# Layer 1's expert results taken back batch by batch inside layer 2's causal attention, and the norms of five attentions computed with GpSimd's power

## The chip, the cores and the metric

The kernel runs on one core of one Trainium2 chip. The metric is the device time of one launch in microseconds, as the median of several runs, and less is better. Each engine of the core (TensorE or PE for matmuls, VectorE or DVE, ScalarE or ACT, GpSimd or POOL, SyncE or SP for DMAs) works off its own instruction queue in order; engines wait for each other through semaphores.

## What is computed

The reference is a post-norm decoder of four layers on `x` of 8 batches x 256 tokens x 256 features, with a context of 8 x 120 x 192. Each layer has a self attention, a cross attention and a feed-forward part, and after each of the twelve parts the residual is added and normalised:

```python
def _layernorm(x, axis=-1, eps=1e-05):
    m = jnp.mean(x, axis=axis, keepdims=True)
    v = jnp.var(x, axis=axis, keepdims=True)
    return (x - m) / jnp.sqrt(v + eps)
...
x = _layernorm(x + _L1_ffn_ref(x, ...), axis=-1)
x = _layernorm(x + _L2_attn_ref(x, ...), axis=-1)
```

Two parts matter here. `_L1_ffn_ref` is a mixture of 32 experts: every token goes to its 4 best experts (256 places each), and gets back the sum of their 4 results times the gate's weights, plus a shared expert's result. `_L2_attn_ref` is a causal attention with 16 heads of 16 features, whose keys and values come from a latent of 64 features behind an exact GELU. The other parts are an attention and cross attentions of other kinds, an expert layer with 8 experts, one with product keys and a table of 4096 experts, a gated convolution, and a feed-forward part on fixed-point numbers (`_L3_ffn_ref`).

## The kernel before

All of `x` stays on the chip as `X`, [128 partitions, 16 tiles, 256]: tile t holds tokens of batch t // 2, so a batch is two tiles. `xT` is its transpose, which the projections read. The twelve parts run one after the other as methods of `Net` (`l0_attn`, `l0_xattn`, `l0_ffn`, `l1_attn`, ... `l2_ffn`; layer 3's parts lie inside `l2_ffn`, the last of them being `fixed_point`, L1438). `build` calls each part's `load_...` one part ahead, so that its weights arrive during the part before, in one of two weight buffers that take turns.

The code states one order of the work. A scheduler in the build places each instruction into its engine's queue, by the program's order and its own estimate of when operands are ready; so the queue order on each engine is fixed before the launch, and where a few parts of the code are independent it can interleave them. Tiles come from pools with a set number of buffers, and a new use of a buffer waits for the readers of the old one.

**The norm.** `finish` (L159) calls `finish_x` (L165) for two tiles, and then `transpose_into_xT` (L150: four PE transposes and an ACT copy). `finish_x` takes mean and variance by `norm_stats` (L141; bn_stats L146 and bn_aggr L147 on DVE), then `rsqrt` (L126), then writes X as (z - mean) * r (L170, DVE). `rsqrt` is an approximation on DVE: add eps (L129), a first guess by integer arithmetic on the float's bits (L131), and three Newton steps of three instructions each (L134, L135, L137). That is eleven DVE instructions on 128x2 elements, each reading the one before. There are 104 norms of two tiles in the program.

**Layer 1's experts (`l1_ffn`, L971).** The gate's scores are ranked, and every token gets four places `slot` and weights `gw` (up to L1039). Each expert then gathers its 256 tokens from DRAM, computes and writes its result to the DRAM tensor `yd` by SP's DMA queue (L1054). In between, `prepare_l2_xattn` puts work of layer 2's cross attention here, including partition all-reduces on POOL. The take-back is the loop after it: for each of 16 tiles a matmul of the shared expert, `acc` = that + X (L1062, DVE), and four gathers of 128 rows of `yd` by `slot` (`gather_rows` L832, an indirect DMA whose descriptors POOL makes, L834) into `yg`, six buffers deep; after each gather DVE adds the row times its weight (L1067). After two tiles, `finish`.

**Layer 2's attention (`l2_attn`, L671, and the `attention16` family).** `attn16_pools` (L374) makes the value buffers `vp` and the row-maximum buffers `low` and fills them by POOL memsets (L384, L387). `attention16` (L571) projects batches in pairs (`pair`, L578: queries, the latent with GELU, keys and values by `project16` L610 and `values16` L405). For each batch, `largest16` (L434) computes scores on PE and reduces them to row maxima on DVE (short rows L445, long rows L461), `lower16` (L474) transposes the maxima and folds them into the queries (L482, DVE), `exps16` (L486) computes the transposed scores and their exponentials (ACT), `sums16` (L538) multiplies by the values and `divided16` (L518) divides; then `project_out` (L561) multiplies by `wo`, adds X plus bias (`biased`, L558, made by POOL, 128x512) into `z` (L566, DVE) and calls `finish_x`. The row maxima of batch b+1 are interleaved with the exponentials of batch b. `l1_xattn` and `l1_attn` use the same functions.

Of the kernel before, what the change touches and what calls it, by code (L numbers as in the profile page):

```python
# [11 lines left out]
F32 = mybir.dt.float32  # L12
BF16 = mybir.dt.bfloat16
I32 = mybir.dt.int32
U32 = mybir.dt.uint32
# [5 lines left out]
P = 128  # L21
# [21 lines left out]
class Net:  # L43
    def __init__(self, ctx: ExitStack, tc: tile.TileContext, ins, out):
# [40 lines left out]
        nc.scalar.dma_start(self.gate1, ins["l1f_gate"].rearrange("p (c n) -> p c n", c=2))  # L85
        self.avg = self.const.tile([P, 2, B], F32, name="avg")
        self.w_scale = self.const.tile([P, len(L2X)], F32, name="w_scale")
        self.wset = 0


# [6 lines left out]
        o, n = LAYOUT.consts[name]  # L97
        return self.consts[:, o : o + n]

    def load(self, *specs, rows=(), flat=None):  # L100
# [4 lines left out]
        total = sum(src.shape[1] for src in srcs) + sum(n for _, n in brow)  # L105
        whole = self.wpool.tile([P, total], F32, name=f"w{self.wset}")
        out, o = [], 0
        for (name, kc), src in zip(specs, srcs):
            part = whole[:, o : o + src.shape[1]]
            self.nc.sync.dma_start(part, src)  # L110
            out.append(part.rearrange("p (c n) -> p c n", c=kc))
            o += src.shape[1]
        for at, n in brow:
            self.nc.sync.dma_start(whole[0:1, o : o + n], self.ins["rows"][:, at : at + n])
            out.append(whole[0:1, o : o + n])
            o += n
        return (out, whole) if flat else out

    def mm(self, out, pairs, bias=None, m=P):
# [4 lines left out]
            self.nc.tensor.matmul(out, lhsT=self.ones[:, :m], rhs=bias, start=False, stop=True)  # L124

    def rsqrt(self, var, n):  # L126
        nc, tmp = self.nc, self.tmp
        v = tmp.tile([P, n], F32, name="rs_v")
        nc.vector.tensor_scalar(v, var, LN_EPS, None, ALU.add)  # L129
        y = tmp.tile([P, n], F32, name="rs_y")  # L130
        nc.vector.tensor_scalar(y.bitcast(I32), v.bitcast(I32), -0.5, 1597463007.0, ALU.mult, ALU.add)  # L131
        for _ in range(3):
            a = tmp.tile([P, n], F32, name="rs_a")
            nc.vector.scalar_tensor_tensor(a, y, -0.5, y, ALU.mult, ALU.mult)  # L134
            nc.vector.tensor_tensor(a, a, v, ALU.mult)  # L135
            y2 = tmp.tile([P, n], F32, name="rs_y")
            nc.vector.scalar_tensor_tensor(y2, a, 1.5, y, ALU.add, ALU.mult)  # L137
            y = y2
        return y
# [231 lines left out]

    def attn16_pools(self, ctx, name, size, nkb):  # L374
        tc, nc = self.tc, self.nc
        pool = ctx.enter_context(tc.tile_pool(name=name, bufs=1))
        work = ctx.enter_context(tc.tile_pool(name=name + "w", bufs=2))
        self.banks = [(ctx.enter_context(tc.tile_pool(name=name + "p", bufs=6, space=PSUM)), "sc")] * 6
        self.banks += [(self.ps_t, "pt")] * 2
        self.next_bank = 0  # L380
        low, vps = [], []
        for n in range(2):
            t = pool.tile([size, 2, nkb, 384], F32, name=f"vp{n}")
            nc.gpsimd.memset(t, 1.0)  # L384
            vps.append(t)
            t = pool.tile([P, 2, 2, P], F32, name=f"low{n}")
            nc.gpsimd.memset(t, 0.0)  # L387
            low.append(t)
        return work, low, vps

# [177 lines left out]

        return project_out, lambda: self.transpose_into_xT(2 * b, 1)

    def attention16(self, project, low, vps, sizes, causal, wo, bo, work):  # L571

# [5 lines left out]
        def pair(b):  # L578
            qv, kv = project(b, vps[b // 2 % 2])
            for n in range(2):  # L580
                q[b + n], k[b + n] = qv[:, :, :, n * S : (n + 1) * S], kv[:, :, :, n * width : (n + 1) * width]

        pair(0)
# [80 lines left out]


    def load_l2_attn(self):
        return self.load(
            ("l2a_wq", 2), ("l2a_wkd", 2), ("l2a_wku", 1), ("l2a_wo", 2), rows=("l2a_bku", "l2a_bo")
        )

    def l2_attn(self, w):  # L671
        nc = self.nc
        wq, wkd, wku, wo, bku, bo = w
        with ExitStack() as ctx:
            work, low, vps = self.attn16_pools(ctx, "a2", P, 2)
            bku, bo = self.everywhere(bku, work, "bku"), self.everywhere(bo, work, "bo")

            def project(b, vp):
# [12 lines left out]
                    self.values16(vp[:, n // 2, n % 2, :], pv, P, bku)  # L691
                return qv, kv

            self.attention16(project, low, vps, [P, P], True, wo, bo, work)

# [275 lines left out]
    def l1_ffn(self, w):  # L971
# [4 lines left out]
        with (  # L976
# [9 lines left out]
            gw = keep.tile([P, NT, K], F32, name="gw")  # L986
            slot = keep.tile([P, NT, K], U32, name="slot")
# [30 lines left out]
            yd = dram.tile([DROP + 1, D], F32, name="yd")  # L1018
# [132 lines left out]
    def l2_ffn(self, w):  # L1151
# [3 lines left out]
        with ExitStack() as ctx:  # L1155
# [760 lines left out]
```

## Time and profile before

| | |
|---|---|
| median of 3 runs | 2713.8 us (2710.76 to 2717.37) |
| the profiled execution | 2858.3 us, of which the profile's span is 2856.3 us |
| busy in the span | PE 2197.9 us (77%), DVE 1778.5 (62%), ACT 929.6 (33%), POOL 843.6 (30%) |
| mean granted TensorE clock | 0.867 of full speed |
| instructions | PE 14323, DVE 6270, ACT 2125, POOL 850 |
| POOL's gathers of `yg` (two expert layers) | 80, 78.4 us, 979 ns each |

The profile is one execution with the profiler on, so it is longer than the runs. A row of instructions gives the line, the engine, the operation, the tiles as out<-in with partitions x elements, the count, and then busy time and the mean of one; what stands after that is the idle time of the engine just before, and in "<-" what ended it. "issue" means that the engine waited for nothing that the profile shows. In a timeline each line is one instruction or several alike, with its start, its length, and in square brackets the idle time before it. The chain of waits is followed back from the last instruction: each line is the piece of work that the next one waited for.

In times of the profile, layer 0's attention runs to about 215 us, its cross attention to 315, its experts to 612, layer 1's attention to 815, its cross attention to 965, its experts to 1330 (routing to 1069, the experts themselves to 1229, then the take-back), layer 2's attention to 1540, its cross attention to 1706, the table experts with layer 3's first parts to 2650, and the fixed-point part to 2856.

### The profile page before, as it was taken

The page shows a single profiled execution, that of the slowest core. Times are in us where ns is not written, and L with a number is a line of the kernel's source. Part 1 is how long each engine was busy: PE and PEld are TensorE (multiplying, and loading weights), DVE is VectorE, ACT ScalarE, POOL GpSimd, SP SyncE. Part 2 cuts the span into 40 slices and gives each one's busy share as a digit, 9 for nine tenths or more (in the row PEclk, how much of TensorE's full clock was granted, in tenths as well). Part 3 has the DMA queues.
Part 4 walks back from the last instruction along what each step waited for, and adds up shares of the span by engine and source line. Part 5 has one row for each costly group of instructions (what it writes and reads, how often), then busy time and mean ns, then how long its engine had stood idle before and what let it go on. Part 6 is the DMA issues. An engine that isn't in the chain of part 4 may idle for free.

```text
span 2856.3 us, 41312 instructions
## 1 busy us (share of the span) xinstructions
PE 2197.9 (77%) x14323; PEld 1590.8 (56%) x14332; DVE 1778.5 (62%) x6270; ACT 929.6 (33%) x2125; POOL 843.6 (30%) x850
## 2 busy tenths in 40 slices
PE   8967587869988858835886667678787787777887
PEld 5544476735555547723554345456576675555665
DVE  4674400066667877445777887476586685755778
ACT  2321132323333302202442153235344344343442
POOL 1010021131111103454010015665656655663000
PEclk9988598989998959967998887789899898888899
DMA  2001266610001015731001011111111111120000
GB/s 79 2 1 37 100 244 238 249 36 1 1 15 53 16 45 153 214 102 45 1 1 56 1 45 34 47 43 40 48 38 45 47 39 38 50 74 19 1 12 19
DMA packets 84175, 166.31 MB, mean 58 GB/s; under 512 B 31654, under 2 KB 51254, under 8 KB 80256
## 3 DMA queue, kind: packets, MB, share of 16 engines
q0 software_dynamic: 52288, 110.52, 12.8%
q1 hardware_dynamic: 26746, 47.35, 5.0%
q10 hardware_dynamic: 4934, 5.82, 0.6%
q8 instruction: 114, 1.87, 0.3%
q14 instruction: 93, 0.76, 0.1%
HBM read 242.90 MB, written 17.70 MB: 91 GB/s over the span
## 4 chain that ended last, share of the span: by engine, by line
PE 24%; DVE 16%; issue 6%; another core or an unknown queue 3%; ACT 2%; POOL 1%; DMA 0%; POOLq 0%; DVEq 0%; ACTq 0%
PE po L1266 5%; PE pp L122 4%; PE s L122 4%; PE po L122 2%; DVE low L461 1%; PE s L1412 1%; PE po L1247 1%; PE s L1390 1%; PE sc L122 1%; DVE junk L1214 1%; POOL rows L834 1%; DVE low L445 1%; PE sc L428 1%; DVE X L170 1%
## 5 line engine op out<-in xcount | busy, mean ns | idle before, releaser
L834 POOL DMA_INDIRECT rows<-in_l2f_table_dram,index x512 | 530.0, 1035 | 364.2 <-issue 107.0
L1266 PE MATMUL po<-rows,diag 128*128 128x256 f32 x768 | 233.3, 441 | 95.4 <-ACT diag L1265 68.1
L1214 DVE SCALAR_TENSOR_TENSOR junk<-rows,X 128x256 f32<-128x256 f32 x512 | 214.9, 420 | 52.5 <-DMA rows<-in_l2f_table_dram,index 25.8
L1266 PEld LDWEIGHTS po<-rows,diag 128*128 128x128 f32 x768 | 156.9, 218 | 147.3 <-ACT diag L1265 80.5
L122 PE MATMUL pp<-xT,w 128*128 128x256 f32 (+1 forms) x672 | 195.6, 432 | 39.6 <-issue 25.3
L122 PE MATMUL ph<-xeT,we 128*128 128x128 f32 x1248 | 188.5, 296 | 41.1 <-DMA we<-in_l0f_experts_dram,wrow 35.9
L122 PEld LDWEIGHTS ph<-xeT,we 128*128 128x128 f32 x1248 | 175.0, 206 | 63.8 <-DMA we<-in_l0f_experts_dram,wrow 39.3
L536 POOL TENSOR_TENSOR aT<-sides,inv 128x256 f32<-128x256 f32 x64 | 46.8, 731 | 518.6 <-DVE sides L534 294.2
L122 PEld LDWEIGHTS pp<-xT,w 128*128 128x128 f32 x672 | 139.9, 215 | 74.4 <-issue 34.4
L156 PE MATMUL pt<-ident,X 128*128 128x128 f32 x352 | 78.1, 337 | 128.5 <-DVE X L170 86.8
L1265 ACT ACTIVATE diag<-ident,dots 128x128 f32<-128x128 f32 x384 | 134.7, 394 | 128.9 <-PE po L1266 57.4
L157 ACT COPY xT<-pt 128x512 f32<-128x512 f32 x88 | 51.6, 586 | 369.4 <-PE pt L156 252.7
L834 POOL DMA_INDIRECT xe<-xd,take x87 | 84.4, 970 | 254.6 <-DVE y L946 101.0
L946 DVE TENSOR_TENSOR y<-py,we 128x256 f32<-128x256 f32 x23 | 9.8, 425 | 226.4 <-PE py L122 226.4
L156 PEld LDWEIGHTS pt<-ident,X 128*128 128x128 f32 x352 | 50.7, 167 | 162.8 <-issue 87.8
L122 PE MATMUL py<-we,hT 128*128 128x256 f32 x496 | 131.6, 390 | 0.9 <-DVE hT L969 0.9
L940 ACT ACTIVATE hT<-ph,we 128x128 f32<-128x128 f32 x184 | 65.8, 367 | 148.4 <-PE ph L122 133.5
L500 ACT ACTIVATE e<-sc 128x512 f32<-128x512 f32 (+1 forms) x148 | 78.6, 602 | 103.1 <-PE sc L428 87.7
L428 PE MATMUL sc<-kv,qv 32*128 32x128 f32 (+2 forms) x1496 | 102.7, 320 | 4.9 <-DVE sides L534 1.8
L428 PEld LDWEIGHTS sc<-kv,qv 32*128 32x128 f32 x1496 | 78.9, 191 | 40.8 <-issue 32.9
L428 PE MATMUL sc<-qv,kv 32*128 32x128 f32 (+2 forms) x1368 | 99.6, 346 | 0.1
L122 PE MATMUL sc<-xT,w 128*128 128x512 f32 x204 | 98.2, 629 | 1.1 <-ACT xT L157 0.7
(458 smaller groups left out, 5170.2 us busy)
## 6 DMA issues: line engine op xcount, KB each, us to landing
we<-in_l1f_experts_dram SPq DMA_DIRECT2D x32, 384.0 KB
yd<-y SPq DMA_DIRECT2D x32, 256.0 KB
rows<-in_l2f_table_dram,index POOLq DMA_INDIRECT x512
xd<-X ACTq DMA_DIRECT2D x16, 256.0 KB
w<-in_l2x_w_dram SPq DMA_DIRECT2D x1, 4096.0 KB
yd<-y SPq DMA_DIRECT2D x23, 128.0 KB
X<-in_x_dram SPq DMA_DIRECT2D x8, 256.0 KB
w<-in_l3f_w_dram SPq DMA_DIRECT2D x2, 1024.0 KB
```

Of the source, the lines that this page charges most:

```text
L122: self.nc.tensor.matmul(out, lhsT=lhsT, rhs=rhs, start=n == 0, stop=n == last and bias is None)
L156: nc.tensor.transpose(pt[:, c, j, :], self.X[:, i0 + j * step, c * P : (c + 1) * P], self.ident)
L157: nc.scalar.copy(self.xT4[:, :, i0 : i0 + step + 1 : step, :], pt)
L170: nc.vector.tensor_scalar(self.X[:, i, :], z[:, j, :], mv[:, j, 0:1], r[:, j : j + 1], ALU.subtract, ALU.mult)
L428: nc.tensor.matmul(sc[: shape[0], part], lhsT=lhsT, rhs=rhs, start=mask is None, stop=True, skip_group_check=True)
L500: lambda r, sc: nc.scalar.activation(e0[m][:n0, r], sc, AF.Exp),
L536: nc.gpsimd.tensor_tensor(out, split(both), split(inv), ALU.mult)
L834: self.nc.gpsimd.indirect_dma_start(out=out, out_offset=None, in_=table, in_offset=bass.IndirectOffsetOnAxis(ap=index, axis=0), **({} if r ...
L940: nc.scalar.activation(hT[:, g + f, :], ph[:, f, :], AF.Gelu, bias=b1[:, g + f : g + f + 1])
L1214: nc.vector.scalar_tensor_tensor(junk, row, 1.0, self.X[:, i, :], ALU.mult, ALU.mult, accum_out=out)
L1265: nc.scalar.activation(diag, self.ident, AF.Copy, scale=dots[:, k : k + 1])
L1266: nc.tensor.matmul(po, lhsT=diag, rhs=rows[:, k, D:], start=False, stop=g + k == H * K - 2)
```

## The change

1. In `l1_ffn` the take-back loop is cut down to the shared expert: eight times, two matmuls into one bank and one DVE addition of 128x512 into X. The gathers, the weighted additions and the norms move to a new method `routed_batches`, whose `batch(b)` does them for one batch, with eight gather buffers in turn instead of six. `attention16` calls it as `ready(b)`: batches 0 and 1 ahead of the first `pair`, batch 2 behind it, and batch b+3 at the head of the loop over b.
2. For this `yd` becomes a DRAM tensor of the whole program, and `gw`, `slot`, the gather buffers and three `z` buffers lie in spare columns of the weight buffer of `l2_attn` (`load(..., spare=...)`).
3. `l2_attn` fills its four buffers by DVE instead of POOL.
4. `rsqrt` gets a second form for the parts in `POWER` and for the fixed-point part: POOL adds eps, and POOL raises to the power -0.5. That holds for 56 of the 104 norms (40 of the five attentions, 8 of layer 1's experts, which are now inside `l2_attn`, and 8 of the fixed-point part).

```diff
     def rsqrt(self, var, n):
+
         nc, tmp = self.nc, self.tmp
+        if self.power:
+            v = tmp.tile([P, n], F32, name="rs_v")
+            nc.gpsimd.tensor_scalar(v, var, LN_EPS, None, ALU.add)
+            y = tmp.tile([P, n], F32, name="rs_y")
+            nc.gpsimd.tensor_tensor(y, v, self.half[:, :n], ALU.pow)
+            return y
...
         for b in range(2 if ready else 0):
+            ready(b)
         pair(0)
+        if ready:
+            ready(2)
         for step in self.largest16(q[0], k[0], low[0], sizes, causal):
             step()
         self.lower16(q[0], low[0])
         before = []
         for b in range(B):
             ahead = []
+            if ready and b + 3 < B:
+                ready(b + 3)
...
-                for i in range(0, NT, 2):
-                    z = work.tile([P, 2, D], F32, name="z")
+                for t in range(0, NT, 2):
+                    po = ps.tile([P, 2, D], F32, name="py")
                     for j in range(2):
-                        t = i + j
-                        po = ps.tile([P, 2, D], F32, name="py")
-                        self.mm(po[:, 0, :], [(shT[:, t * P : (t + 1) * P], sd)])
-                        acc = work.tile([P, D], F32, name="acc")
-                        nc.vector.tensor_tensor(acc, po[:, 0, :], self.X[:, t, :], ALU.add)
-                        for k in range(K):
-                            y = work.tile([P, D], F32, name="yg", bufs=6)
-                            self.gather_rows(y, yd, slot[:, t, k : k + 1])
-                            out = z[:, j] if k == K - 1 else acc
-                            nc.vector.scalar_tensor_tensor(out, y, gw[:, t, k : k + 1], acc, ALU.mult, ALU.add)
-                    self.finish(i, 1, z)
+                        self.mm(po[:, j, :], [(shT[:, (t + j) * P : (t + j + 1) * P], sd)])
+                    x = self.X[:, t : t + 2, :]
+                    nc.vector.tensor_tensor(x, po, x, ALU.add)
+
+    def routed_batches(self, spare):
+
+        nc = self.nc
+        zs = spare[:, : 6 * D].rearrange("p (n j d) -> p n j d", n=3, d=D)
+        ys = spare[:, 6 * D :].rearrange("p (n d) -> p n d", d=D)
+        state = {"turn": 0}
+
+        def batch(b):
+            z = zs[:, b % 3]
+            for j in range(2):
+                t = 2 * b + j
+                for k in range(4):
+                    y = ys[:, state["turn"] % ys.shape[1]]
+                    state["turn"] += 1
+                    self.gather_rows(y, self.yd1, self.slot1[:, t, k : k + 1])
+                    acc = z[:, j] if k else self.X[:, t, :]
+                    nc.vector.scalar_tensor_tensor(z[:, j], y, self.gw1[:, t, k : k + 1], acc, ALU.mult, ALU.add)
+            self.finish(2 * b, 1, z)
+
+        return batch
...
+            self.power = True
             self.fixed_point(w4, pool, work, ps)
...
+POWER = ("l0_attn", "l0_xattn", "l1_attn", "l1_xattn", "l2_attn")
...
+            net.power = name in POWER
             getattr(net, name)(w)
```

Of the 14 x 256 columns that `routed_batches` gets, the first six are the three `z` buffers, and the other eight are the gather buffers.

More of the change, by code (lines that the diff above doesn't have):

```diff
@@ L87, in __init__ @@
         self.w_scale = self.const.tile([P, len(L2X)], F32, name="w_scale")
+        self.half = self.const.tile([P, 2], F32, name="half")
+        nc.gpsimd.memset(self.half, -0.5)
+        self.power = False
+        dram = ctx.enter_context(tc.tile_pool(name="dram", bufs=1, space=bass.MemoryType.DRAM))
+        self.yd1 = dram.tile([32 * 256 + 1, D], F32, name="yd1")
         self.wset = 0
@@ L98, in cst, with load @@
         return self.consts[:, o : o + n]
-    def load(self, *specs, rows=(), flat=None):
+    def load(self, *specs, rows=(), flat=None, spare=0):
         self.wset ^= 1
@@ L104, in load @@
         brow = [LAYOUT.rows[name] for name in rows]
-        total = sum(src.shape[1] for src in srcs) + sum(n for _, n in brow)
+        total = sum(src.shape[1] for src in srcs) + sum(n for _, n in brow) + spare
         whole = self.wpool.tile([P, total], F32, name=f"w{self.wset}")
@@ L116, in load @@
             o += n
+        if spare:
+            out.append(whole[:, o:])
         return (out, whole) if flat else out
@@ L364, in l0_xattn, with attn16_pools @@
                 self.finish(2 * b, 1, z)
-    def attn16_pools(self, ctx, name, size, nkb):
+    def attn16_pools(self, ctx, name, size, nkb, fill=None):
         tc, nc = self.tc, self.nc
+        fill = fill or nc.gpsimd
         pool = ctx.enter_context(tc.tile_pool(name=name, bufs=1))
@@ L383, in attn16_pools @@
             t = pool.tile([size, 2, nkb, 384], F32, name=f"vp{n}")
-            nc.gpsimd.memset(t, 1.0)
+            fill.memset(t, 1.0)
             vps.append(t)
             t = pool.tile([P, 2, 2, P], F32, name=f"low{n}")
-            nc.gpsimd.memset(t, 0.0)
+            fill.memset(t, 0.0)
             low.append(t)
@@ L569, in sums16, with attention16 @@
         return project_out, lambda: self.transpose_into_xT(2 * b, 1)
-    def attention16(self, project, low, vps, sizes, causal, wo, bo, work):
+    def attention16(self, project, low, vps, sizes, causal, wo, bo, work, ready=None):
         width = S if causal else SC
@@ L581, in pair @@
                 q[b + n], k[b + n] = qv[:, :, :, n * S : (n + 1) * S], kv[:, :, :, n * width : (n + 1) * width]
+        for b in range(2 if ready else 0):
+            ready(b)
         pair(0)
+        if ready:
+            ready(2)
         for step in self.largest16(q[0], k[0], low[0], sizes, causal):
@@ L666, in load_l2_attn @@
     def load_l2_attn(self):
-        return self.load(
-            ("l2a_wq", 2), ("l2a_wkd", 2), ("l2a_wku", 1), ("l2a_wo", 2), rows=("l2a_bku", "l2a_bo")
-        )
+        *w, spare = self.load(
+            ("l2a_wq", 2), ("l2a_wkd", 2), ("l2a_wku", 1), ("l2a_wo", 2), rows=("l2a_bku", "l2a_bo"),
+            spare=14 * D + 8 * NT,
+        )
+        both = spare[:, 14 * D :].rearrange("p (a t k) -> p a t k", a=2, k=4)
+        self.gw1, self.slot1 = both[:, 0], both[:, 1].bitcast(U32)
+        return *w, spare[:, : 14 * D]
     def l2_attn(self, w):
         nc = self.nc
-        wq, wkd, wku, wo, bku, bo = w
+        wq, wkd, wku, wo, bku, bo, spare = w
         with ExitStack() as ctx:
-            work, low, vps = self.attn16_pools(ctx, "a2", P, 2)
+            work, low, vps = self.attn16_pools(ctx, "a2", P, 2, nc.vector)
             bku, bo = self.everywhere(bku, work, "bku"), self.everywhere(bo, work, "bo")
@@ L692, in project @@
                 return qv, kv
-            self.attention16(project, low, vps, [P, P], True, wo, bo, work)
+            self.attention16(project, low, vps, [P, P], True, wo, bo, work, self.routed_batches(spare))
     def load_l1_attn(self):
@@ L985, in l1_ffn @@
             nc.sync.dma_start(sd, self.ins["l1f_sd"])
-            gw = keep.tile([P, NT, K], F32, name="gw")
-            slot = keep.tile([P, NT, K], U32, name="slot")
+            gw, slot, yd = self.gw1, self.slot1, self.yd1
             with tc.tile_pool(name="f1q", bufs=1) as pool:
@@ L1017, in l1_ffn @@
             pool = ctx.enter_context(tc.tile_pool(name="f1l", bufs=1))
-            yd = dram.tile([DROP + 1, D], F32, name="yd")
             none = pool.tile([1, D], F32, name="none")
```

## The prediction

> **What bounds the kernel now.** I began with the page's busy shares (PE 77%, DVE 62%, POOL 30%): no engine fills the span, so the sum says little and I cut the span at the stages. The windows view answers with span, then busy time per engine (PE, PEld, DVE, ACT, POOL), then the granted TensorE clock. Six rows, one per stage that the change touches:
>
> ```profile
> 172.00:215.00 43.00, 25.18 (x86) 17.30 (x85) 31.73 (x144) 4.03 (x7) 7.60 (x6) 0.72 0.00 1
> 215.00:315.00 100.00, 73.23 (x247) 45.24 (x246) 46.66 (x197) 18.34 (x65) 0.30 (x1) 0.72 0.11 35
> 612.00:815.00 203.00, 185.45 (x1676) 110.64 (x1676) 136.77 (x335) 72.20 (x127) 31.81 (x31) 0.96 0.01 1
> 815.00:965.00 150.00, 125.69 (x1289) 85.33 (x1292) 113.98 (x319) 54.06 (x104) 20.87 (x25) 0.91 0.10 36
> 1229.00:1330.00 101.00, 30.56 (x70) 14.23 (x70) 55.38 (x217) 7.84 (x13) 66.54 (x68) 0.54 0.30 84
> 1330.00:1540.00 210.00, 176.57 (x1938) 109.37 (x1939) 150.49 (x386) 82.89 (x145) 21.74 (x24) 0.98 0.02 7
> ```
>
> They are layer 0's attention tail, layer 0's cross attention, layer 1's attention and cross attention, the take-back of layer 1's experts, layer 2's attention. The fifth is a hole: PE works 31 of 101 us. POOL's timeline says who fills it:
>
> ```profile
> 1229.37 0.95 POOL L834 DMA_INDIRECT yg<-yd,slot  x1 [11.64 <-DMA yd<-y]
> 1230.62 0.95 POOL L834 DMA_INDIRECT yg<-yd,slot  x1 [0.30 <-issue]
> ...
> 1317.31 0.95 POOL L834 DMA_INDIRECT yg<-yd,slot  x1 [0.30 <-issue]
> 1326.28 1.38 POOL L384 MEMSET vp<- 128x1536 f32 x1 [8.02 <-DVE X L170]
> ...
> 1336.54 2.49 POOL L558 TENSOR_TENSOR biased<-X,bo 128x512 f32<-128x512 f32 x2 [6.62 <-issue]
> ```
>
> 64 gathers 1.25 us apart (0.95 plus 0.30 of issue) take 1229.4 to 1318.3. The take-back is bound by GpSimd's gathers, and attention starts behind the last. The last line matters later: 6.62 us in which POOL waits for nothing shown, ahead of its first ordinary operation after the partition all-reduces.
>
> In the attentions the chain of waits runs through the norm:
>
> ```profile
> 1451.28 0.75 DVE ln_st L146 x2
> 1452.03 0.23 DVE ln_mv L147 x2
> ...
> 1452.28 0.42 DVE rs_v L129
> ...
> 1454.49 0.17 DVE rs_y L137
> ...
> 1454.69 0.74 DVE X L170 x2
> 1455.42 2.41 DVE low L461 x4
> ```
>
> Eleven 2-element instructions, each waiting for the one before, hold DVE 2.41 us (1452.28 to 1454.69), and the next batch's reduces start the moment X is done: nothing covers it.
>
> **The norms by power.** Removed per norm: 2.41 us (2.2 in the last norm of the fixed-point stage, 2850.23 to 2852.40). Added: two hops and two POOL operations. DVE end to POOL start was 0.17 (1516.08 to 1516.25), a POOL operation on the one before 0.17, POOL to DVE 0.04 (1546.47 to 1546.51). The eps addition: the POOL additions take 0.73 us for 256 elements and 1.27 for 512, which is 0.19 + 2.1 ns per element, so 0.2 for two. The power, p, is in no row. From below: 0.11 (the 8-wide memset). From above: 1.27 (the 512-wide addition). It works on two elements, so I put it nearest to the small rows, the all-reduce's 0.31 to 0.38: p = 0.3. New path 0.17 + 0.2 + 0.17 + 0.3 + 0.04 = 0.9; full saving 1.5.
>
> The Trainium skill (GPSIMD Engine Reference, 4.1 Engine selection) speaks against it: elementwise work belongs on VectorE, GpSimd being about 2x slower for two inputs. By the rule, two operations of 2 x 0.19 beside the hops make 1.14 us, still half of 2.41: the rule compares one operation with one, here two replace eleven. I take the rows.
>
> How much of 1.5 reaches the end:
> - Layer 0's attention: eight norms in the tail, two batches interleaved, so about 1.0 each: 8.
> - Layer 0's cross attention: X comes 3.14 us after the aggregate (260.05 to 263.19), other DVE work between; PE's transposes wait 2.67 for it each batch. 3.14 - 0.9 = 2.2, less some wait on PE: 1.9 x 8 = 15.
> - Layer 1's attention: 1.4 x 8 = 11. PE has 18 us of slack there (203 - 185), so it doesn't take over.
> - Layer 1's cross attention and layer 2's own norms: POOL's `biased` (1.27, starting with z's end, 1451.39 to 1452.66) stands ahead of the eps addition and costs 0.3 to 0.4: 1.25 x 8 = 10 each, 20 together.
> - Fixed-point stage: the chains cost about 8 (three waits of 3.3, 1.15 and 2.2, the others interleaved at 0.1): two thirds, 5.
> Sum 59. One more us of p costs about 45 us (not 56: some norms interleave).
>
> **The take-back.** Its 64 gathers, 64 additions and 8 norms now stand inside layer 2's attention, in the order that the built program gives each engine. POOL: 18 gathers, a reload, two norms with a gather between, on to gather 32, the norm of batch 2, on to gather 64 with the norms of batches 3 and 4; with eight buffers a gather waits for the addition 8 before. DVE: 18 additions, X of batches 0 and 1, the first projections, and then additions mixed among them. An addition that waits for its gather blocks all of DVE's queue behind it. So I walked both queues on before's clock, gather 1 at 1229.37.
> - Gather 18 ends 1252. Then POOL needs its reload: in before the 6.62 above, hidden under projections; here the norms of batches 0 and 1 stand behind it. The Trainium skill (GPSIMD Engine Reference, 2.1 Instruction dispatch) puts the first call to a freshly loaded kernel at about 6 us; the rows are 5.76, 5.96 and 6.62, and I use 6.5 (by the page the sum would be half a us better). Power done 1260.9, X 1262.2, first query matmul 1264.5 (before: 1320.1). So far 56 us are won.
> - Then they go back. Addition 27 stands ahead of the first projection's copies (gather landed 1272.6), 36 ahead of the keys (1286.4). Additions 45 to 57 stand behind batch 0's lower scores (done 1310.4), so gather 53, which waits for addition 45, starts only at 1311. Eleven more at 1.25: gather 64 starts 1324.8, lands 2.8 later, its addition ends 1328.1. All of that stands ahead of batch 1's long reduces. Eight of them take 5.2, so batch 1's lower scores are done at 1334.8. In before that was 1361 (L482 at 1359.65 + 1.41). Gained: 26.
> - The X of batches 5 to 7 still come later in the attention, each next to an own norm, about 1.9 each: 6 back. Net 20.
>
> What else moves. Four memsets leave POOL (3.8 us: 2 x 1.38 + 2 x 0.53) for DVE, which idles for the first gather (4.18 us): nothing; uncovered, at most 4. The shared expert: 16 additions of 0.4 become 8 of about 0.7, under the last experts' y: nothing, uncovered below zero (0.8 less). SP's queue is unchanged. On POOL the gathers are moved past `biased` and the norms; they run 1.04 to 1.23 beside a busy DVE, not 0.95, which if all did would add 64 x 0.15 = 10. The gathers' landing (2.8 us from start to the addition, 1229.37 to 1232.20) is covered by eight buffers at 1.25 each, 10 us, as long as DVE takes its additions at once.
>
> **Sum.** 59 + 20 = 79 us of the profiled execution: 2858.3 (span 2856.3 and 2 around it) to 2779. That execution is 5.3% above the runs' median of 2713.8, so I scale by 2713.8/2858.3 = 0.9495: 2639 us.
>
> **Rivals.**
> - *The power is dear*, p = 1.0, near the upper row. For: a power is more than an addition, and the fixed part is only bounded by rows of other operations. 79 - 0.7 x 45 = 47: 2811 x 0.9495 = 2669.
> - *The attention swallows the gathers.* If the DVE waits above overlap with work that PE has to do anyway, the 56 us of the early start stay, less the 6: take-back 50. For: PE is the busiest there (177 of 210). Against: DVE's order. 59 + 50 = 109: 2611.
> - *Nothing is hidden*: the attention still ends its first scores where the gathers end, reload on top (-6.5). 59 - 6.5 = 52: 2664.
> - *GpSimd's queue becomes the norm path (slower).* Every norm's power waits in one in-order queue behind `biased`, `aT` divisions and 64 gathers, and if the power itself runs as a slow routine of several us, all 48 attention norms lengthen. At 45 us per us, it turns at p = 0.3 + 79/45 = 2.1; at p = 3 it is 2858 + 43, scaled 2754. Against it: no POOL row of that width is over 0.4.
>
> **How the numbers follow.** Likeliest as summed, 0.50; dear power 0.20; swallowed 0.15; nothing hidden 0.10; GpSimd's queue 0.05. 0.2%, or 5 us, is about what a measurement of this kernel can tell from no change. A gain under that needs p near 2: 0.02 of the dear case goes to same, so faster 0.93, same 0.02, slower 0.05. The range takes in the dear power and nothing hidden with some us for slower gathers (2690), and the swallowed case with a cheap power at p = 0.11, 0.19 x 45 x 0.95 = 8 below 2611 (2600).
>
> **What would show it.** Right: power rows on POOL of about 0.3 us; 0.9 from the aggregate's end to X; the first query matmul of layer 2 some 35 us after gather 1 starts, not 91; a POOL gap of 6 to 7 us after gather 18; DVE's additions ended by gathers in between the attention's reduces; from gather 1 to the end of layer 2's attention 311 - 20 - 10 = 281 us of profile. Wrong: power rows over 1 us; PE waiting for X in layer 0's cross attention as long as now; or a PE clock that falls once the hole is closed (granted 0.54 in it, 0.98 after it), which would take back part of every matmul behind and which I put at nothing.

## The result, and the profile after

| | median us | ratio to before, 95% interval |
|---|---|---|
| before | 2715.59 | |
| changed kernel | 2684.35 (2682.18 to 2689.11, 4 runs) | 0.989 (0.987 to 0.991) |
| forecast | 2639 | 0.972 |

The change gains 31 us where 75 were forecast; 2684 us lies near the slow end of the forecast's range (2600 to 2690). The kernel before, run beside each group of kernels below, took 2714 to 2720 us in three groups and 2851 and 2854 in two, for a cause that no run shows (one chip, number 7, is in both kinds), so ratios, and differences inside one group, are what compares.

The changed kernel's profiled execution took 2683.91 us, its span 2682.1. The same six stages in its windows view (busy time of PE, PEld, DVE, ACT, POOL, then the granted clock), the fifth being the 101 us from gather 1 on:

```profile
172.00:206.00 34.00, 20.66 (x74) 14.30 (x72) 16.97 (x53) 4.08 (x7) 14.34 (x22) 0.75 0.00 0
206.00:292.00 86.00, 69.94 (x248) 42.41 (x246) 34.00 (x113) 18.29 (x65) 7.70 (x17) 0.80 0.12 40
592.00:817.00 225.00, 207.65 (x2042) 126.94 (x2042) 143.80 (x296) 85.16 (x153) 44.72 (x56) 0.99 0.01 4
817.00:967.00 150.00, 124.28 (x1246) 84.25 (x1244) 109.33 (x264) 55.73 (x106) 29.40 (x41) 0.89 0.12 44
1180.00:1281.00 101.00, 46.82 (x269) 26.38 (x271) 59.68 (x134) 13.58 (x21) 69.82 (x76) 0.66 0.30 84
1281.00:1475.00 194.00, 166.98 (x1744) 101.97 (x1736) 124.99 (x288) 77.62 (x136) 29.31 (x44) 0.94 0.02 5
```

The hole is partly filled (PE works 47 us in it, not 31), the cross attention of layer 0 is 14 us shorter. But the last row's clock is 0.94 where it was 0.98. The norm in layer 2's attention, in the chain of waits:

```profile
1391.13 0.61 DVE z L582
1391.74 0.07 issue
1391.81 1.27 POOL biased L574
1393.08 0.20 POOL rs_v L139
1393.27 0.07 issue
1393.35 0.72 POOL rs_y L141
1394.07 0.03 issue
1394.09 0.73 DVE X L185 x2
1394.83 2.41 DVE low L477 x4
```

From z's end to X it is 2.35 us, against 3.44 before (1451.25 to 1454.69 in its chain). `biased` is now a link of the chain, as forecast. From the aggregate's end (1392.73 in DVE's timeline) to X it is 1.36 us. The forecast had 0.9, and 1.2 to 1.3 where `biased` stands ahead. The power takes 0.715 us on average, as the groups say, where the sum had 0.3.

```profile
L185 DVE TENSOR_SCALAR X<-z,ln_mv,rs_y 128x256 f32<-128x256 f32 x176 | 65.9, 417 | 50.7 <-POOL rs_y L141 50.6
L141 POOL TENSOR_TENSOR rs_y<-rs_v,half 128x2 f32<-128x2 f32 x56 | 40.0, 715 | 14.8 <-DVE rs_y L152 10.5
```

POOL's timeline of the take-back:

```profile
1179.90 0.94 POOL L860 DMA_INDIRECT w<-yd,w  x1 [12.33 <-DMA yd<-y]
...
1201.43 0.95 POOL L860 DMA_INDIRECT w<-yd,w  x1 [0.30 <-DVE ln_mv L162]
1209.92 0.43 POOL L139 TENSOR_SCALAR rs_v<-ln_mv 128x2 f32<-128x2 f32 x2 [7.54 <-issue]
1210.53 1.19 POOL L860 DMA_INDIRECT w<-yd,w  x1 [0.17 <-issue]
1211.75 1.56 POOL L141 TENSOR_TENSOR rs_y<-rs_v,half 128x2 f32<-128x2 f32 x2
...
1278.20 1.10 POOL L860 DMA_INDIRECT w<-yd,w  x1 [0.30 <-DVE w L1102]
```

The idle time that the prediction calls GpSimd's reload stands where it was forecast, behind gather 18, and takes 7.54 us, not 6.5. The last gather starts 98.3 us behind the first (forecast: 95.4).

And a place where nothing was forecast to go wrong, PE's timeline at the end of the fixed-point stage, where `ph` are a chunk's first matmuls and `po` its last:

```profile
2636.67 3.62 PE L130 MATMUL po<-w,v 128*128 128x256 f32 x16
2640.22 0.69 PE L132 MATMUL po<-b,ones 1*128 1x256 f32 x2
2640.84 3.72 PE L130 MATMUL po<-w,v 128*128 128x256 f32 x16
2644.49 0.69 PE L132 MATMUL po<-b,ones 1*128 1x256 f32 x2
2645.12 0.70 PE L130 MATMUL ph<-xT,w 128*128 128x256 f32 x2
2662.50 5.76 PE L130 MATMUL po<-w,v 128*128 128x256 f32 x16 [16.68 <-DVE v L1511]
```

The last chunk's final `ph` stand behind the chunk before's `po` in PE's queue. Only then can ACT and DVE work on that chunk, and PE idles 16.68 us for them.

### The profile page after: what moved, and what is told of

It is laid out like the page before. It is cut to its first block, busy times and chain, and to the rows that moved or that the text cites. A ratio compares the mean times of both kernels' runs of the same rounds, so it can differ in the third digit from the quotient of the medians.

```text
span 2682.1 us, 40785 instructions
## 1 busy us (share of the span) xinstructions
PE 2159.7 (81%) x14332; PEld 1568.1 (58%) x14332; DVE 1694.7 (63%) x5650; ACT 931.4 (35%) x2125; POOL 898.0 (33%) x959
## 4 chain that ended last, share of the span: by engine, by line
PE 30%; DVE 24%; DMA 9%; issue 6%; POOL 5%; ACT 3%; POOLq 0%; ACTq 0%; DVEq 0%
DMA rows<-in_l2f_table_dram,index 6%; PE sc L130 3%; PE ph L130 3%; PE pp L130 3%; PE po L130 3%; DVE low L477 3%; PE po L1304 2%; PE s L130 2%; DVE low L461 2%; PE sc L444 2%; DVE junk L1252 2%; DMA xe<-xd,take 2%; POOL rows L860 2%; DVE X L185 1%; DMA w<-yd,w 1%
## 5 line engine op out<-in xcount | busy, mean ns | idle before, releaser
L1304 PE MATMUL po<-rows,diag 128*128 128x256 f32 x768 | 216.6, 420 | 39.3 <-ACT diag L1303 39.0
L1304 PEld LDWEIGHTS po<-rows,diag 128*128 128x128 f32 x768 | 148.2, 206 | 86.1 <-ACT diag L1303 59.7
L130 PE MATMUL pp<-xT,w 128*128 128x256 f32 (+1 forms) x672 | 187.7, 418 | 11.3 <-DVE hT L995 4.3
L130 PEld LDWEIGHTS pp<-xT,w 128*128 128x128 f32 x672 | 133.2, 205 | 43.0 <-issue 7.4
L139 POOL TENSOR_SCALAR rs_v<-ln_mv 128x2 f32<-128x2 f32 x56 | 14.2, 254 | 400.9 <-DVE ln_mv L162 365.4
L172 ACT COPY xT<-pt 128x512 f32<-128x512 f32 x88 | 51.5, 587 | 271.4 <-PE pt L171 270.8
L444 PE MATMUL sc<-kv,qv 32*128 32x128 f32 (+2 forms) x1496 | 108.2, 332 | 4.6 <-DVE sides L550 1.7
L516 ACT ACTIVATE e<-sc 128x512 f32<-128x512 f32 (+1 forms) x148 | 78.6, 602 | 93.0 <-PE sc L444 77.4
```

The lines of the kernel that those rows point to most:

```text
L130: self.nc.tensor.matmul(out, lhsT=lhsT, rhs=rhs, start=n == 0, stop=n == last and bias is None)
L172: nc.scalar.copy(self.xT4[:, :, i0 : i0 + step + 1 : step, :], pt)
L444: nc.tensor.matmul(sc[: shape[0], part], lhsT=lhsT, rhs=rhs, start=mask is None, stop=True, skip_group_check=True)
L516: lambda r, sc: nc.scalar.activation(e0[m][:n0, r], sc, AF.Exp),
L1304: nc.tensor.matmul(po, lhsT=diag, rhs=rows[:, k, D:], start=False, stop=g + k == H * K - 2)
```

## The experiments

My theory after the profile: the attentions' norms gain what they should, the fixed-point stage loses about 16 us through PE's order, and the take-back gives back what it wins. The rivals: the stage differences are accidents of single profiles; GpSimd's way itself costs; the take-back is worth 20 us and something else loses.

**The parts, one by one.** First the kernel before itself, profiled again (e0).

> The kernel before, unchanged, profiled a second time. Theory: the first profile of before was long (2858 us against a median of 2714) in the table-expert stage alone, which took 949 us there and 819 in the changed kernel though its queues have the same order; a second profile shows that stage near 805 us and a span near 2713, and all other stages as in the first. Rival: the profiler slows this program as a whole, so the span is near 2856 again and the stage near 949.

It took 2716.34 us, ratio 1.0013 (0.9991 to 1.0035). Its profiled execution took 2707.39, span 2705.4, less than the median: it isn't the profiler that made the first profile 2858 us long. The theory held for the table stage; "all others as in the first" held but for the take-back, and for some 7 us in the stages ahead of it. The windows view of that stage, first profile and second:

```profile
1706.00:2650.00 944.00, 725.21 (x3160) 563.01 (x3160) 609.17 (x2980) 371.15 (x959) 532.76 (x514) 0.86 0.17 43
```

```profile
1688.00:2500.00 812.00, 693.89 (x3163) 539.62 (x3162) 609.41 (x2983) 371.54 (x959) 534.43 (x514) 0.91 0.19 50
```

DVE, ACT and POOL did the same work; 132 us are waiting. ACT's waits in the first profile show some of it, eight stalls whose releaser the trace doesn't know ("remote"), up to 13.9 us long (total us, times, longest); they aren't among the second's longest waits:

```profile
ACT silu L968 <- remote: 44.4, 5, 12.3
ACT qT L1207 <- remote: 30.2, 3, 13.9
```

The 64 gathers, too, took 88.9 us there and 80.0 here. So the forecast's profile was no stretched copy of the runs: nearly all of its surplus lay in one stage, and some 9 us in the gathers.

Newton back in the fixed-point stage alone (e1):

```diff
-            self.power = True
+            self.power = False
             self.fixed_point(w4, pool, work, ps)
```

> The changed kernel with Newton's norm back in the fixed-point stage alone (PE's queue there is then that of before again). Theory: the power there moves the next chunk's first matmuls behind the chunk before in PE's queue and costs 16 us against before, so this run is 16 us faster than the changed kernel: about 2668. Rival: those 16 us are an accident of one profile and the power saves 5 there as forecast, so this run is slower: about 2689.

2665.99 us, ratio 0.9821 (0.9794 to 0.9848): 18 us faster than the changed kernel. PE's order is that of before again, and the last wait on DVE is half as long. These lines are from the trace of the same kernel run once more (e1b below); e1's own has the same 8.84:

```profile
2632.84 3.72 PE L130 MATMUL po<-w,v 128*128 128x256 f32 x16
2636.49 0.69 PE L132 MATMUL po<-b,ones 1*128 1x256 f32 x2
2646.03 6.00 PE L130 MATMUL po<-w,v 128*128 128x256 f32 x16 [8.84 <-DVE v L1511]
```

The stage, from ScalarE's first `v` to the end of the program, took 220.3 us in the changed kernel's trace, 201.8 in e1's and 201.4 in e0's.

The take-back alone (e2: e1 with `POWER = ()`), and the power alone (e3: the kernel before with `rsqrt`'s new form and `POWER`):

> The changed kernel with Newton's norm everywhere: the take-back inside the attention and the memsets alone. Theory: the take-back brings some 20 us (gather 1 to batch 1's lower scores fell from 132 to 112 us), a few more since GpSimd's reload is off the path without the power, a few less since DVE carries the routed norms: 2690 to 2700. Rival: the take-back brings nothing and all of the gain is the norms': 2714.

> The kernel before with the power in the five attentions alone, no take-back, Newton in the fixed-point stage. Theory: the stages of the first four attentions fell by 8.6, 14.9, 13.3 and 9.3 us, which is 46, and layer 2's own norms bring 7: about 2661. Rival: part of that is the difference between two profiles, and the norms bring 1.1 us less each for DVE's time only where DVE is the last: about 2690.

The take-back alone: 2715.07 us, ratio 0.9998 (0.9981 to 1.0015), the rival's number. The power alone: 2663.80, ratio 0.9803 (0.9774 to 0.9833), the theory's. Beside it e1, which is the same and the take-back, is 2665.99. So the five attentions' norms are worth 50 us (45 to 61 by the interval). The take-back is worth nothing that these runs can tell, with the power or without (without it, at most 5 us either way).

**Where the take-back's gain goes.** The traces show when each batch's lower scores are done (end of its second L482, L498 after), in us behind gather 1; the last column is the attention's last X. The runs c1, d1b and t1 come further down.

| run | batch 0 | batch 1 | batch 4 | batch 7 | end |
|---|---|---|---|---|---|
| before, first profile | 116.6 | 131.7 | 213.0 | 284.9 | 310.5 |
| before, second | 107.3 | 121.4 | 202.8 | 274.6 | 300.2 |
| power alone (e3) | 108.7 | 126.1 | 204.2 | 272.2 | 295.1 |
| changed kernel | 83.4 | 112.3 | 203.5 | 271.4 | 295.3 |
| e1 | 83.0 | 111.9 | 204.4 | 272.3 | 294.8 |
| take-back alone (e2) | 79.4 | 105.0 | 200.1 | 275.5 | 300.6 |
| c1, late norms out | 84.7 | 113.5 | 193.7 | 261.6 | |
| d1b, early reload | 78.6 | 103.2 | 195.8 | 263.8 | 286.3 |
| t1, gated | 63.2 | 94.1 | 207.5 | 283.5 | 306.0 |

Batch 1 is 14 us ahead in e1 against e3; at batch 4 nothing is left. The steps between show it: 29.6, 19.6 and 28.9 us in e3, 33.6, 24.7 and 34.2 in e1. With Newton's norm (e2 against the second profile of before) the same three steps lose as much, 95 us against 81. In these three steps stand the routed norms of batches 5 to 7. The run c1 leaves them out:

```diff
-            self.finish(2 * b, 1, z)
+            if b < 5:
+                self.finish(2 * b, 1, z)
+            else:
+                self.transpose_into_xT(2 * b, 1)
```

> The changed kernel with Newton in the fixed-point stage, and the routed norms of batches 5 to 7 left out (statistics, power and the writing of X; the gathers, the weighted additions and the transposes stay). Theory: of what the early start won, the steps between batch 1 and batch 4 lost 13 us, since three routed norms were moved out of the gathers' hole into a stretch that DVE bounds; without them 11 to 13 us come back: about 2654. Rival: the steps are longer because of the interleaving of queues or the clock, not the norms' own work: 2663 to 2666.

2771.49 us where before took 2850.65, ratio 0.9731 (0.97 to 0.9762). That time doesn't answer the question: the same replacement stands in two more places of c1's kernel, so the norms of batches 5 to 7 are left out in two later parts too, and no e1 was run beside it. The trace up to the end of the attention does: the steps are 29.9, 20.2 and 30.1 us, nearly those of e3, and batch 7 comes 10.7 us earlier than in e1. Of the 14 us that the three steps lost, 12 go with the moved norms. One of them in DVE's timeline of the changed kernel, the routed X (`X<-w`) right behind an own one (`X<-z`):

```profile
1313.49 0.73 DVE L185 TENSOR_SCALAR X<-z,ln_mv,rs_y 128x256 f32<-128x256 f32 x2 [0.83 <-POOL rs_y L141]
1314.14 0.24 DVE L162 BATCH_NORM_AGGREGATE ln_mv<-ln_st 128x2 f32<-128x6 f32 x2
1315.51 0.73 DVE L185 TENSOR_SCALAR X<-w,ln_mv,rs_y 128x256 f32<-128x256 f32 x2 [1.13 <-POOL rs_y L141]
```

Work of about 1.9 us, and a wait of 1.13 for the second power in a row: 3 of the 4 to 5 us per step. PE's clock differs too. Windows of 80 us from 120 us behind gather 1, e3, then e1, then c1:

```profile
1298.66:1378.66 80.00, 72.29 (x761) 43.61 (x762) 54.25 (x123) 37.06 (x62) 10.93 (x15) 1.00 0.01 1
```

```profile
1297.76:1377.76 80.00, 70.22 (x672) 43.13 (x671) 49.20 (x120) 32.50 (x55) 12.27 (x19) 0.89 0.01 1
```

```profile
1306.09:1386.09 80.00, 73.29 (x809) 46.26 (x810) 52.95 (x119) 36.94 (x64) 10.85 (x15) 1.00 0.01 2
```

In e1 PE is granted 0.89, and is busy 104 ns per matmul record instead of 95 (e3). With the norms out it is 1.00 again, but the norms don't fix it: in f2b (below), which has the same attention, the same window shows 0.97, and there the three steps take 88 us, where e1 takes 92.5 and e3 78. So about 4 of the 14 us go with the clock and 10 with the norms' own work and waits, as far as one such trace tells.

**The reload.** An ordinary 2-element GpSimd operation in the experts' loop (d1):

```diff
+                    if e == E - 2:
+                        early = self.tmp.tile([P, 2], F32, name="rs_v")
+                        nc.gpsimd.tensor_tensor(early, y[:, 0, :2], self.half, ALU.mult)
```

> The changed kernel with Newton in the fixed-point stage, and one ordinary 2-element GpSimd operation after the expert before the last, so that GpSimd's reload (7.54 us behind gather 18) falls into its wait for the last expert's result. Theory: what comes first in the attention starts 7 us earlier and keeps 4 to 7 of it: 2659 to 2662. Rival: the gathers' stream and the additions ahead of batch 1 set the end, and the reload is covered by them: 2665 to 2667.

2779.02 us, ratio 0.9772 (0.9741 to 0.9803), without e1 beside it. So both once more, side by side (e1b and d1b):

> The changed kernel with Newton in the fixed-point stage once more, as the anchor on the same chip for the runs beside it. Theory and rival alike: a ratio to before of 0.972 to 0.983, as the chip has it.

> The anchor with GpSimd's reload moved into its wait for the last expert's result, once more beside its anchor. Theory: 5 to 9 us faster than the anchor (its lower scores of batch 1 came at 106 us behind gather 1, against 112 and 115, and its attention kept 8 of that). Rival: within 2 us of the anchor.

The anchor: 2666.61, ratio 0.9817 (0.9797 to 0.9837). Early reload: 2661.05, 0.9776 (0.9759 to 0.9794), 5.6 us faster; the intervals only just part. POOL's timeline shows the reload's 7 us ahead of gather 1, where POOL waits anyway:

```profile
1182.17 0.18 POOL L1079 TENSOR_TENSOR rs_v<-y,half 128x2 f32<-128x2 f32 x1 [7.01 <-DVE hT L995]
1186.78 1.19 POOL L860 DMA_INDIRECT w<-yd,w  x1 [4.42 <-DMA yd<-y]
...
1209.51 0.27 POOL L139 TENSOR_SCALAR rs_v<-ln_mv 128x2 f32<-128x2 f32 x1
```

**The additions held back.** On top of the early reload, batch b+3's weights get 0 times batch b's row maxima added, which puts its additions behind batch b's reduces (t1):

```diff
...
+                m = behind[:, 1, 1, :8].rearrange("p (t k) -> p t k", k=4)
+                nc.vector.scalar_tensor_tensor(g, m, 0.0, g, ALU.mult, ALU.add)
```

> As the run with the early reload, and a gate: the gate's weights of batch b+3 get the row maxima of batch b times zero added, so that its eight additions stand behind batch b's reduces in DVE's queue instead of all 64 ahead of batch 1's. Theory A (additions that wait for gathers ahead of batch 1 hold up the attention): batch 1's lower scores come 15 to 25 us earlier, and since 40 additions (16 us) and five routed norms (3 us each) then stand among DVE-bound work, about 5 to 10 stay: 5 to 10 us faster than the early reload alone. Theory B (DVE and PE bound the attention so closely that every us of moved DVE work costs a us): no gain, within 3 us or slower.

2676.43 us, ratio 0.9859 (0.9838 to 0.988), 15 us slower than d1b. Batch 1 is 9 us earlier, and by batch 4 it is 12 late. With eight buffers the gathers then stop too:

```profile
1242.74 1.07 POOL L860 DMA_INDIRECT w<-yd,w  x1 [16.29 <-DVE w L1109]
```

So my theory A fell: the earlier start doesn't stay. That the moved work alone costs this isn't shown, since GpSimd's in-order queue stands in the way as well. The powers of routed batches wait behind gathers there, and from gather 1 to the attention's end DVE waits 43.3 us for powers, against 32.9 in d1b:

```profile
1286.65 0.95 POOL L860 DMA_INDIRECT w<-yd,w  x1 [0.30 <-issue]
1287.62 0.24 POOL L139 TENSOR_SCALAR rs_v<-ln_mv 128x2 f32<-128x2 f32 x1
1287.94 0.72 POOL L141 TENSOR_TENSOR rs_y<-rs_v,half 128x2 f32<-128x2 f32 x1
```

```profile
1288.70 0.41 DVE L185 TENSOR_SCALAR X<-w,ln_mv,rs_y 128x256 f32<-128x256 f32 x1 [4.55 <-POOL rs_y L141]
```

**The fixed-point stage: order or GpSimd?** The first matmuls written one chunk ahead, with power (f1) and with Newton (f2):

```diff
-        for o in range(0, NTOK, T):
+        def project(o):
...
+            return v
+
+        ahead = project(0)
+        for o in range(0, NTOK, T):
+            v = ahead
+            if o + T < NTOK:
+                ahead = project(o + T)
```

> The changed kernel (power in the fixed-point stage too), with that stage's first matmuls written one chunk ahead in the program, so that PE's queue has 12 or more of the next chunk's before each chunk's last matmuls. Theory (queue order is what cost 18 us, not the power): the loss is gone, about 2662 to 2668. Rival (the way over GpSimd itself costs it, its 1.3 us[...]): still near 2684.

> The same reordered fixed-point stage with Newton's norm there. Theory: the order is as good as before's, so 2666 as in the run with Newton and the old program; against the reordered run with power it is up to 5 us slower, the saving of 1.1 us in at most four exposed norms. Rival: if GpSimd's way costs, this one is faster than the run with power by 10 or more.

With power 2783.37 us, ratio 0.9795 (0.9763 to 0.9828); with Newton 2776.90, 0.9754 (0.9728 to 0.9781). The 6 us between them lie within the scatter of the first (2778 to 2803). So the pair once more (f1b and f2b):

> Once more, beside its pair: the changed kernel, power everywhere, the fixed-point stage's first matmuls one chunk ahead. Theory (the 18 us were PE's queue order, and the power itself is worth little there): within 5 us of the run with Newton beside it, and some 18 faster than the changed kernel (ratio to before about 0.982 where the changed kernel's is 0.989). Rival (GpSimd's way itself costs): 10 or more slower than the run with Newton.

> The same with Newton in the fixed-point stage. Theory: 5 to 9 us faster than with Newton and the old order (ratio about 0.979), since the reordered stage took 7 to 9 us less in two profiles. Rival: no faster than the old order, 0.982.

2795.34 us, 0.9781 (0.9755 to 0.9808), and 2793.64 us, 0.9795 (0.9772 to 0.9818): equal within their intervals. The traces are sharper. The stage, counted as above, takes 198.6 and 199.0 us with power and 194.7 and 194.8 with Newton (f1 and f1b, f2 and f2b). So with the power kept and the order changed, 21 of the changed kernel's 220.3 us are gone: the order it was. The power saves nothing there; its stage is still 4 us longer than Newton's, though the built orders of the two differ a little as well, so that the 4 us have no one cause shown. PE's last wait on DVE, f1b and then f2b:

```profile
2778.64 6.65 PE L130 MATMUL po<-w,v 128*128 128x256 f32 x16 [8.17 <-DVE v L1518]
```

```profile
2763.19 6.35 PE L130 MATMUL po<-w,v 128*128 128x256 f32 x16 [5.70 <-DVE v L1518]
```

The reordered stage with Newton is also 7 us shorter than the old order with Newton (201.4 to 202.0 in eleven traces), but f2b's ratio of 0.9795 doesn't show this in the whole time.

**The slope of the norm.** A second power (to 1.0) behind the first in e3 (k1), and in e3 the eps addition moved to DVE (h3):

> The run with the power in five attentions alone, and a second power (to 1.0) behind the first: 0.71 plus a GpSimd hop of 0.17, which is 0.88 us more on each of 40 norms. Theory A (the forecast's slope, 45 us of time per us of power for 56 norms, so about 40 for these): 35 us slower than with one power, ratio to before about 0.993. Theory B (the power's time is partly covered, and the norms gain for another reason, DVE's freed time): 10 to 20 us slower, ratio 0.984 to 0.988.

> The run with the power in five attentions alone, with the eps addition on DVE, where it follows the aggregate in 0.02 us and takes 0.16 to 0.2, not on GpSimd behind the bias addition: some 0.2 us less per norm. Theory A: 8 us faster than with the addition on GpSimd, ratio about 0.977. Theory B: within 3 us, ratio about 0.980.

A second power: 2701.58 us, ratio 0.995 (0.9931 to 0.997). That is 40 us above e3's ratio, and 32 us above h3, which was measured beside it. X's wait from the aggregate's end, one norm of layer 1's attention, in e3 and then in k1, shows what was added, 0.77 us and not 0.88:

```profile
672.52 0.74 DVE L179 TENSOR_SCALAR X<-z,ln_mv,rs_y 128x256 f32<-128x256 f32 x2 [1.13 <-POOL rs_y L135]
```

```profile
690.90 0.74 DVE L182 TENSOR_SCALAR X<-z,ln_mv,rs_y 128x256 f32<-128x256 f32 x2 [1.90 <-POOL rs_y L138]
```

On 40 norms that is 31 us, and all of it reaches the end: theory A. What 40 us have above 31 isn't shown; k1's granted clock was 0.01 to 0.04 lower than e3's in the four attentions behind the first.

The addition on DVE: 2669.95, 0.9822 (0.9798 to 0.9846), nothing gained. Its trace says why. In layer 1's attention the same wait fell from 1.13 to 1.01 us, in layer 0's attention it grew, and over the 40 norms the way from aggregate to X sums to 51.4 us, against 50.8 in e3.

**Putting it together.** The parts combined, with the gate (b2), without the take-back (b1), and with the take-back and the early reload (d2):

> The gated kernel with the eps addition on DVE (only the power on GpSimd), and the reordered fixed-point stage with Newton. Theory: 0.2 us less on 48 norms, of which some 35 are exposed, is 7, and the reordered stage is 2 to 8 faster: 8 to 14 us faster than the gated kernel, the fastest of all. Rival: the addition on DVE costs DVE what it saves on GpSimd: only the fixed-point part shows, 2 to 8.

> No take-back change: the kernel before with the power in five attentions, the eps addition on DVE, and the reordered fixed-point stage with Newton. Theory: 50 us from the norms, 5 to 7 more from the addition on DVE, 7 from the order: ratio about 0.976. Rival: the addition on DVE gives nothing: 0.978.

> The changed kernel with the early reload, the eps addition on DVE, and the reordered fixed-point stage with Newton. Theory: the take-back with the early reload is worth 6 to 8 us, so this one is 6 to 8 faster than the run without the take-back beside it: ratio about 0.973. Rival: the take-back is worth nothing even then, and both are equal.

The gated one: 2668.88 us, ratio 0.9816 (0.9795 to 0.9837), 7.5 faster than t1 beside it, which is within its rival's 2 to 8, and not the fastest: d1b beside it took 2661.05. The other two were measured beside f1b and f2b. No take-back: 2794.15, 0.9796 (0.9774 to 0.9817), which takes in its rival's 0.978 and not its theory's 0.976. Take-back with the early reload: 2782.52, 0.9748 (0.9726 to 0.9771), 12 us faster than that, where 6 to 8 were expected. f2b, which has the take-back without the early reload (and eps on GpSimd), was 2793.64: no gain again. So the take-back is worth something once GpSimd's reload is off its path, in this group. There the 64 gathers ran slowly (88.3 us in b1, 80.3 in e3), so there was more to hide; where they run in 80 us, no pair was measured. d2 has the lowest ratio of all complete kernels, but its interval overlaps that of f2 (0.9754) and d1b.

## Why the prediction was wrong, point by point

The forecast of 75 us in runs was 51 for the attentions' norms (54 of profile), 5 for the fixed-point stage, and 19 for the take-back (20 of profile). Measured: 50, -18 and about 0.

- **Attention norms: 51 forecast, 50 measured, and the agreement is luck in part.** "It works on two elements, so I put it nearest to the small rows ... p = 0.3" failed: the power takes 0.71. (Two of the all-reduces in the same profile took 0.45 and 0.49, above the 0.38 and the 0.4 named.) "Removed per norm: 2.41 us" was too much for some: in layer 1's attention the way from the aggregate's end to X was 2.21 us in e0 and 1.13 in e3, in layer 1's cross attention 2.44 and 1.36. So a norm that stands alone in the chain saves 1.08, not the "full saving 1.5", and the 36 full savings in the sum would be 39 us. By stages (e0 against e3, from a stage's last X to the next one's) the norms brought 7.6, 12.8, 9.7 and 13.2 us in the first four attentions, and 5.1 in layer 2's from gather 1 to the end, where 8, 15, 11, 10 and 10 were forecast. Why layer 1's cross attention gained more than its eight norms' 8.6, and layer 2's less, isn't shown.
- **Fixed point: the step that failed is "two thirds, 5".** It priced the norm's latency and assumed that the queues stay as they are. The build gave PE another order; this is fixed ahead of the launch, but the prediction compares no queue of PE's in that stage. Measured 18 us the other way (e1), and gone when the program restores an order with the next chunk's first matmuls ahead (220.3 us of stage, 198.6 and 199.0 in f1 and f1b).
- **Take-back: "Gained: 26" failed in its baseline.** The walk itself nearly held. The first query matmul was forecast 35.1 us behind gather 1 and came at 35.9, batch 0's lower scores at 81.0 and came at 83.4, batch 1's at 105.4 and came at 112.3. In these last 7 us are the reload (1 more), the dearer powers, gathers that end 3 later and a wait of 2.46 for PE ahead of the last reduces. But the gain was counted against a profile with slow gathers, in which batch 1 took 131.7 us; the second profile of before has 121.4. That leaves 9.
- **"about 1.9 each: 6 back" was too small.** What the moved routed norms take back is 12 us (c1). Their work of 1.9 us each was right, but each also waits for a second power on GpSimd. And PE's clock in that stretch, which the prediction named as a sign of being wrong and "put at nothing", fell from 1.00 to 0.89 in e1, and that is about 4 us of it.
- **Scaling by 0.9495** spread a surplus over all stages that lay mostly in one. It made the forecast smaller by 4 us, so it hid part of the error.
- Right were the chain's order (`biased` ahead of eps), the reload's place, DVE's additions as the blocker ahead of batch 1 (t1 moved them, and batch 1 came 9 us earlier), and that the slower rival (a power of 2.1 us and more) did not come about.

Of the rivals, "nothing is hidden" came nearest for the take-back, by another way: the hiding happens, and is given back. The dear power came true in part, 0.71 of its 1.0.

## What to carry to other kernels

A chain of eleven dependent two-element operations can be worth handing to another engine even at 0.7 us for the one that replaces it, if nothing covers the chain: count the whole path with its hops, and measure how much of it reaches the end by lengthening it. Work moved out of a hole into a stretch that is bound elsewhere has to be priced there, with its waits and what they do to the other engines. And an edit to one small operation can change the built order of instructions that it doesn't touch: compare the whole queues of each stage, and where they differ, walk the stage again.

## What the runs showed of the hardware

- GpSimd's power on 128x2 elements: 0.707 us at the median, three times the addition beside it (0.217).
- Ahead of GpSimd's first ordinary operation behind the partition all-reduces stand 7.54 us in which it waits for nothing shown (6.62 before). They leave the path when one small operation comes earlier, in an idle stretch (d1b).
- PE's granted clock over the same 80 us of layer 2's attention was 0.89 in e1, 0.97 in f2b and 1.00 in e0, at 70.22, 67.96 and 70.14 us of PE busy. So PE's busy share doesn't decide it; what does was not tried.
- The same instructions took 944 us in the table-expert stage of one profile and 812 in another, with ACT stalls of up to 13.9 us in the first whose cause the trace doesn't show, and 64 gathers took 88.9 and 80.0.
